# Sums of four pairs of states, new slot counts and a new order in a layer of attention, experts and a state-space mixer on Trainium2

## The chip, the cores and the metric

The kernel runs on one core of one Trainium2 chip. A core has five engines with a queue of instructions each: PE (matrix products, with PEld for the loading of weights beside it), DVE (vector), ACT (scalar), POOL (GpSimd) and SP, which here only issues DMA transfers. 16 DMA engines move data between the chip's main memory (DRAM) and the on-chip memory SBUF; PE writes its results to a second on-chip memory, PSUM. The metric is the time of one execution on the device, in microseconds (us); lower is better.

## The reference

The input x has 16 sequences of 256 tokens of 128 numbers. Four sublayers follow, each added to x:

```python
x = x + attention(layernorm(x), w_in, b_in, w_out, b_out)
x = x + ffn(layernorm(x), gate_w, w1, w2)
x = x + mixer(layernorm(x), W_x, W_dt, b_dt, A_log, D, W_out, b_out)
x = x + ffn(layernorm(x), gate_w, w1, w2)          # the same weights again
```

In `attention` the softmax weights `att[b, l, m, h]` sum to 1 over m, and they are used in `einsum('blmh,blhd->blhd', att, v)`, where nothing else depends on m. So only v, w_out and the biases matter.

`ffn` sends each token to the two best of 8 experts:

```python
top_vals, top_idx = top_k(x @ gate_w, 2)
top_w = softmax(top_vals)
h = relu(einsum('td,edf->etf', x, w1))             # 128 -> 512
expert_out = einsum('etf,efd->etd', h, w2)         # 512 -> 128
final = einsum('etd,te->td', expert_out, combine)  # combine: top_w at the two experts
```

`mixer` is a selective scan with 16 states n per channel d. With delta, B and C made from x by products with W_x and W_dt:

```python
dA_cumsum = exp(sum over later positions of delta * A[d, n])
xs = cumsum(delta * u * B[n] * dA_cumsum) / (dA_cumsum + 1e-12)
y = sum over n of xs * C[n] + u * D
out = y @ W_out + b_out
```

All is in 32-bit floats.

## The kernel before

The 4,096 tokens are cut into eight blocks of 512 (`TB`). A block goes through attention, the gate, its experts, the mixer, a second gate, its experts and the output. For the experts the blocks are put together in sets: in the first layer [0], [1], [2,3], [4,5], [6,7] (`FIRST`), in the second [0,1], [2,3], [4,5], [6], [7] (`SECOND`).

**Routing.** For each set, a buffer `slots` in DRAM has room for `SLOTS` tokens per expert: the first number of a layer's tuple for a set of one block, the second for a set of two. `route` counts each token's place in its expert, and POOL scatters the weighted rows there with indirect transfers (L807). If an expert had more tokens than there is room for, a general version of the whole computation would run after the planned one (`general`, behind a branch at the end). With the reference's inputs the fullest expert has 142 tokens in the single sets of layer 1, 310 in the double ones, 318 in the double sets of layer 2 and 176 in the single ones.

**Experts.** `divided` turns the room into chunks: at most 128 tokens to a chunk, all chunks of one size. 330 tokens are 3 chunks of 110. For each expert of a set, `experts` fetches its tokens from `slots` as a tile `xs` of [chunk, number of chunks, 128] with one transfer from SP's queue. It transposes them on PE to `xsT`, does four products with `w1_s` into the banks `ps_b`, relu on ACT or DVE into `h`, four products with `w2_s` into `ps_y`, transposes back and stores `yr` in the buffer `ys` in DRAM with another transfer from SP's queue. There are four buffers each for `xs` and `yr`. Every row that such a transfer moves is 512 bytes long. So each layer has 40 fetches and 40 stores. When a set's stores have landed, POOL gathers the rows for each token into `yy` (`collect`, L821), and they are added to x.

**Mixer.** One call does a block. For each pair of states, ACT makes `decay` and `th` (two exponentials and tanh for the two states, 512 columns each), PE spreads B and C over the partitions into `ps_B` and `ps_C` from three bf16 pieces, DVE multiplies (`ps_B`), scans (`w`) and multiplies with C and `w` into `th`, which holds two states of 512 columns:

```python
            group.append(th)
            if len(group) > 1:
                product(group[0], group[0], th, ALU.add)
            if len(group) == ADD:
                for k in range(2):
                    matmul(so, wsh_s, group[0][:, k, :], False, n + k == NS - 1)
                group = []
```

With `ADD` = 2, two such tiles are added up on POOL or DVE and then multiplied with W_out (`wsh_s`) into the bank `ps_s`: four groups in a block, 8 products of 512 columns. A product of 32-bit floats shows as two records on PE.

**The order.** Nothing here is issued in the order of the program text. Every operation becomes a job of a `Plan`, with the engines that may do it (`either` offers two for many: POOL or DVE for `product`, ACT or DVE for copies and relu) and an assumed duration from `cost`, `matmul`, `transpose` or `move`. `Plan.forward` plays the jobs through with these durations, picks by a rank for each job, which the packed string `ORDER` holds, and so decides the engine, the buffers and the place of each instruction. What comes out is a fixed sequence for each engine. The engines then follow their sequences, each waiting on semaphores for what it needs. All operations made by these helpers carry L710 in the profile.

Of the kernel before, what the change touches and what calls it, by code (L numbers as in the profile page):

```python
# [40 lines left out]
XN, ROW, XS, XT, H, YT, DEPTH = 4, 3, 4, 3, 4, 3, 3  # L41

ORDER = (
    "c-oy;3zS?{m92a3_kHWtzxw}AcS6!hI-~;z$O;57;6V8Q2_u0S5d^_uSc)<WMU9}iM3yW-9GO9x!6gH;R9KFnMgszpL;?f?f"
    "k*<R^Xq@t@4Y*x(n)u9Rdv$gbywAU_uY5jJ?HGR&pu3!7%XbbZAPKv1@3dL7-PWr9y>~ce89&%(C@K%Jo9!(hVu?i`7ck&TU"
    "=}!eF%Vl)_8eOGlzoV+GCP40*uyj))&`!j{^V`L0}L96gZ<4gs;O)2b>A*3(6>rA1qHftKE)g1PD&+d4C53zj>tYtuRmST4)"
    "&WZ=i;-Wdt8&k}Jkz4frZfW0dx>2F9<qDP7bBq>YMzaZlQu8;l;?+ePSH#x<oKoEc04YdQ9_z#2UcR8YkQZ@_JKUIwrXpCBw"
    "y%n$|z+H*Fet87`^C*_nH1fcC_oYqiEa5-i%s&Llw`v@46X#t7>ItB=v6B`tD>z8D<E*H}0f-#>loAIJY14hsV+|<5QxV>F6"
    ">MACb|KehA*xQaiirRK`r;~{cLjneDt0Nf|kEoo*U@p9_j!i#dWsezvrR+sxshv)zuWsGhFh-7pml~U+|6RMg#e{BnBi1OJ8"
    "{AtKz1A~GTIhQXQRn%ke_1+;3-()<bWZJRR6xkpvtH^UoJyCT1TFBd-vKZw{l=N5^8I7n;k;oMd;@Ct0ds)?$Q&UmPXz}F6#"  # L50
    "dW9?-*SWOvxor10@uUMTT|4)h($^?t#9+p%<8@UwC4u_H&;{uTgXsAMiMbl@4dSA0RXZ4ACKM^vhG!qIZ3nF^_^|>`d-Tn&K"
    "wyzk<LlLQRB1Sh~zY_bopU;AF}%AS(s#+{Wm8iwK;{49U2`nGz1AY|+UEUrmJ%G;LyF9NZ`WH88wyQ>luGWVmKT3OV<!#{EW"
    "z!NIr5>A!W@A}UR$AWI|yFk+BEncN=R!(&QNPwlz&?wY>(L5$Xj@WkfMZ5@g#l8cWfdX#yell3CZhJqETdv4Sl?uKS~-)v})"
    "*4Vd22ckBKk|8VVy=0BLVS=}uE1S@ZYfgCSgm>u8<lgqPqc<;kc?rNJurWMKMhvbR2qEm+|2UcJKs<96Vvpuj0d3D4Ol{~jD"
    "cbd9cbIWM858=Cz7YhCRBII%{;(YO>*0hKYgrutqLc+%P%RBi3%*?jzD0>I3<3Efd@<bwI+I<3KauaD-H2gE37^e)@TEs7Rl"
    "mCTe(M@e{Hq2=o>!CxJnq#en9mpN*lS+&Iw2j!+`ts4{f2PVMHH#yYYq^BZsi=|-|t8(JfC6;{iqKJpA{YQK>8{db}Y7%1%m"
    "$WPD1#pR5Rju3=MF*JyEdPx|=W?&I655)808;G9f7ezWWA3XfwvOg@aHMUvd&5l5TnkS>p^$u;L$4aYP5jbo}#ADG_H0DKuj"
    "u!Z7tjkurLfov96nM^nzTX@8{Q$937vRW0C-5uOb^Oj3%l#B4<#!j~c5E#e_fwC;J+RCpwK|NPft1JPleU~<FVRNIdf6eaz_"
    "Nv0P>Z+A!CEICH}&6*u~1??PyUf7eg8@uY%b;<r%k|>f-k1T$sZg1Me)YxXVdWNeW?%8tuHdp{3#ogBbYA;w0bivzZvubm=S"
    ";u|tWYNdXxF6B#=HHK)3%~O5?RK;+SsOX+qgTI%sagY#bZ33c{lh?fXeo(UeK9XlQ!l>}&R7jB33OpT{afUf*+^D_6L!6*c<"  # L60
    "h7L9m@!!-^s_fy|QfmDvDt?3h}Vp{*$OLDcCS%nsc8svmPfsu)&;TDFcKF;EU}a@<8*34~xXDg|A}%sHpKTeo9dE`>kiXNE!"
    "2}Rao~0CdHr>Vh5vv;!0oyH0!d8k45OvgXmyL7+J<Yl^FG(U|O>XL3Z^p+mWlK0Gj2vl>bFE98-Xh<|d<ttXm_ycw_46$d*="
    "N{H*TW<G$1MvHzy|X*oCAKl|_DUET4E2{EZ~6~SV(+hdkJ2eiw&E}+CZo)u}D7<-j8X)h}#*5`2TRY(d%ak`I(om3YX7XQ;-"
    "82r-(aOFxjFT(DFH3&d<{WUmyg<*(gK;*T8E51PH6`c5O%$++arQY0k=N}_YL3^ZMXC|Hk8Tkp7kug{EMoc)KVA>SNEd*jOR"
    "9YC!pixRCZz|TuC8>TjE2Sd2j>|k}_jex`*77FX%xVN5;iP64HL+aT94Q(>1jRGe9_6W#Uzmtbw}b7x^s&|tS_9HVKCt5A<r"
    ";K3#2~{Q$LJJ~Hs`_xjttq@*ZSwWyjf2SC@AZj@tRoMK)SD!2#kI>vgzGf`??{<_J?ayD>|GN-@g6sACYC`O>cGby6Yag{&{"
    "i}+$XP#SP|(-qF~Kw%fXLgv}ls@Vcf(y{7%z2MX{bU?!9o?c~7re&u%04nm5av&iTz*iXBTg#+qYc$6S5>Z_diGZg@Lf6Z@l"
    ")wW4G;Y_;oS5sUq}{^J@BankP?#tvB!n0-i|(&S41wf@8QeqzI@v|6^xKn>E_@SbQwN(5yWll87$l4ZQ+dV~^R$DnXlPzYRo"
    ")nh#23O4sr7AdIyNKVav-OU8V&iXsz8B^JL-v%twpAwQ=Qp|pL-T}0+fY4v3M`J_Ct2}NOAeM^U#$*H;)v^arT5v56Py~LZy"
    "KtG#Z#A8=wV{w6{Aq2UK4;F$;&&I4XD{lhb2fGEE&R*a#-{EVssn+QktixhOrgXABzgXo6auRe$x$=KXq4BsUH~Xp{8b1kln"  # L70
    "N+6lChLhmik8mt@M}Y;tMZR#K=n$X_u5IpFss8+P{mW+v!LiI0f_TD5d!MEHHWJ{fMhI2>AeM8WT~lFC&MDJMTtfyM<#FVQG"
    "6lvYlzEg5Xy?ijwILJC0%|7jEaAdM4HQ9Ul^>ZtxO2d*7_vQ`_~SaB^+CfzpN?51RLemBMwz*BO@dmSRRDbMiV)Q)90R8v)z"
    "PHZ9pW?~U#))Iqb7HGfO(OYbK0V2jtFoI3HtT9vb*jfliR`xD_|=fpUst#pJqUfuD|?7`1i9dy4PmcQ6C_ua2TI`NL#X@*mg"
    "FRefEuh)`e$Qz<7@yzC)%_k#wz7<VN(?nT?jN!h38#$$@B&A}fNhKD)_V3C>6?W_Km;UG4d2i226s4(^Prc~oj9DzqGETcK8"
    "l1I%Z`po^mmqr`!`l4Z+3U}RBpKnhl}a~$D~2#N!gR!o$meVKHLX;2^h2XY87cFhMkAv)*fxxquK9mk7i_+QICRJ`ksSbxqM"
    "*I8qi^KK9B8|S>`kad*b*wWhc}`O7B-;)d)e~yQKVGI!z@(HG(2T0$>Pb^WShXEOR;`2lv#Y9kQb>_Ogj2i=fq_yU67CeVZr"
    "{@gsGEVbJj_oU$d>DPTCh!;?-g}h~-P|d6M0v5E0K_4$xYQ1gxnot`W$KR~PH@`L`l|7UC;<sTQxWUQ6||poTy22!i!IhKzy"
    "pXQf3l-Gg!A-@Dv~rsY^rO)gVE@UZZmD)VdP0}msHuac5QY{JGYJL#qvpHEjmiedOSa1F&HY|ulVc)O@cHts`I{@eiBjwR(!"
    "_8ix^k!l0(h~&T7vM4e5KVN*DYOK3E+dhbWdb3?O^7)&A1eAW?=7Vz!2K8hi*_g1DL}BPd81oY)3j%rzwa6$#het4-Ihzya7"
    "77H$j6raj9Caxc6jsy)rla2BZ#kLR!ussM?-TivyE_K=-%6eQ%Dy}IKPmF8KGQE(BPY{&sD0aUkypJowK$5&pz3Zxld!;r4b"  # L80
    "i{@8#QJ_IFn*;{VzcdLVpURg@j=$V-dy;p8g9$&<0E*5r}RnW4ssP!0vkwhv!q5M?mqtJQ-&7z$ANdJr>3`CNU5J!(3K065A"
    "i+L-$}&JeEnTAef=kA}-sw&-e>J#HChX&52<yMomPBiDcydpfxkF<esn+mybj<nYg@AEfou;>8oatI$$gl&*zUTVA&_w=>d0"
    ")VuxalN-e>{1?hHd#T<gEY603Sq;ya#Gqh_Mm3NVtcv12paWEAp@N;jl_QKli;?LCjg<s`!{TB$IU6ISyA=LpWVI7x57}ZFu"
    "UyR@ii5A&vj>Y+kR=nMcOp1blceu7K&ZmLJKbnmXE#R8F_*sih9<z#X+;A%6{A{Ez$^$XzqzsgPamGSd;v$zQUxv|TBU}pJO"
    "amc?{~0On8j*%t>`(S5uz_(gF0ig2eO`~@C)l`YfsL7i$mXvUPy{QQMzyN>t{N*$*BV(<B)RH{Zi?qJ-47zZD6A6QTNl6PX5"
    "ISpC}NRp5Pnd{WL_F(JZ&*EA26kJwh%tbQBz`jL{MqK*a1OmW2Y&=;)dCIpY+M<9hn6WW0SGk%=for-_rsND|HXUrYeDY^Wt"
    "uRc9iXm1sqF%8mqwdiz%BgB3yFq0D1xK{)d$SD=|z!!`R#$kn*RmVr&^uNvVT^94rO$#9JszL!=M5ANyV03eex*#vqAJ5%Ny"
    "4jqAju=(&N=4uCL$VU#40LZNbPG?#1NILG;DwkqZqSz2uCi;rN@$1`Lu><|JJbQm8p-oY1<G0KV!2gME%*-8+W+2sVI7iO}V"
    "by#4#`*ZG+D5_>`9E(B_QH4OGPsRbTmB)28Dj{m%J|AhKbS}aVhfpCwQ3T%8MPLEt0_hZ!m=-&iwY`GPJ764^K~`KA)|>;ZT"
    "@}ro$BSFRTs>(OgIUG3@gF-FYys&tR|0K7L5=Q1R;Acpqk2X^1mlt)<4r;#9V#Ar;xBaY8bA8LwH`k|bnD=W9={Cqp~?6mho"  # L90
    "&4_Wy<Nnt3%6`4o`d?Jc7`~W)6IU(A0xWeYE66moHm&C{%Swf1)8>zM4L0V)e(guDC4q`lQj5u0A+aaZ8un3Qd1Ymv1sxdPR"
    "bXpF`2ny4=hvZmZ(jB1TFvQ!y*3d@871G&uZwjyQCLcvtak_0a06QK|H{u2@M=iF$eXLNf~A_>t8mIX5}CBwCXxTAHI}2I<h"
    "`E~}xkx}PS^I0)w{z$;7M(mMgE@bH1*P=z1LhC|cMJ}fL|GOVkadMHZ|Iwe#A`toNgp%6N%#M5OoJ7Xx|oBi^Al<r1{j)cBY"
    "l~?L1sL<2Fxe}N<G+K_!DGWB1<tAJ`9fwY^rJe?ox=L6Hjs_FgT9+F+bp=uascEUaWHugt_1Qsn0t`Y``6H-EgwhO|E(3LFi"
    "Z?4fSLUZ9QdC9!r$s_l{2aE7_!YHqVmIU{%F`z!%!=I%kKZ5%&Cmzc%b~}~q>IM!rb81tqy!K!VUCYqq#7$!!==bhCX=3s;$"
    "%^*;wCa3OO-O9o(ZQ-hqNQio)L;mia^O(WxDCmOmSION~THP!{KuJTjQtx^z2P$M2bgM$Pd4pP-rZqEAXmI7_yZA^bv5zLiv"
    "(<9@0~Uc6m5-C3WfQIGd(iPb1aJH#rlw)TN|RU9cU3796-NOrQ-8{Em$WuY$d&)W2z2U6(ZvewlXCrKM0GRTY^=ugp-!=%Y&"
    "Fsu8My`l0<!hGyKW_?@eYMLo3~SMyobTC68?dK%$h)m{3q^-@n)MyH}zA67bsj(WIKz)be3x{NFe<qcAG^{A`%9Fy8f&&*3R"
# [1408 lines left out]
```

## Time and profile before

| | |
|---|---|
| time, median of 9 runs | 794.86 us |
| lowest and highest | 791.75 and 800.44 us |
| the profiled execution's own time | 793.23 us |
| its span, first to last instruction | 791.5 us |
| mean granted clock of TensorE | 0.885 |

The profile is of one execution. Its page gives the busy time of each engine, the DMA queues (q1 is SP's, q0 that of POOL's indirect transfers), the groups of instructions (line, engine, operation, output<-inputs, shapes, count, busy time in us, mean duration in ns, idle time before them and what ended it) and who waited for whom. A table of stretches gives, for any two moments, the busy time and number of instructions of each engine, the granted clock, the mean busy share of the 16 DMA engines and the GB/s that they moved. A timeline lists the instructions in order of time: start, duration, engine, operation, count.

### The profile page before, as it was taken

The numbers are of one execution on the slowest core, as the hardware profiler recorded it, in microseconds if no ns is written. First come the engines' busy times: TensorE is split into PE (matmuls) and PEld (weight loads), VectorE is DVE, ScalarE is ACT, GpSimd is POOL, SyncE is SP. The second block draws the span as 40 slices with busy tenths as digits, with TensorE's granted clock in tenths as the row PEclk, the third lists the DMA queues.
The fourth block names the chain that finished last, engine by engine and source line by source line (L and its number), as shares of the span: only waits on it lengthen the run. The fifth ranks groups of instructions, "written<-read, shape, count | busy, mean of one in ns | idle before, by whom it ended". The sixth has DMA issues, their size and how long they took to land. (4 is left out here: it accounts for less than half of the span.)

```text
span 791.5 us, 8786 instructions
## 1 busy us (share of the span) xinstructions
PE 647.5 (82%) x2598; PEld 402.3 (51%) x2598; DVE 555.2 (70%) x1038; ACT 487.5 (62%) x996; POOL 414.5 (52%) x490
## 2 busy tenths in 40 slices
...
GB/s 242 330 50 59 76 79 34 61 47 60 77 76 18 9 18 49 109 61 34 27 69 82 46 20 64 21 59 40 35 50 90 123 41 70 65 59 96 43 94 96
DMA packets 76373, 55.05 MB, mean 70 GB/s; under 512 B 8064, under 2 KB 69152, under 8 KB 76320
## 3 DMA queue, kind: packets, MB, share of 16 engines
q1 hardware_dynamic: 66464, 37.35, 16.2%
q0 software_dynamic: 8192, 16.79, 7.2%
...
q14 instruction: 31, 0.25, 0.1%
...
## 5 line engine op out<-in xcount | busy, mean ns | idle before, releaser
L710 PE MATMUL ps_b<-xsT,w_s 128*128 128x330 f32 (+3 forms) x640 | 221.2, 456 | 34.5 <-issue 14.0
L710 PE MATMUL ps_y<-h,w_s 128*128 128x330 f32 (+3 forms) x640 | 218.1, 431 | 7.2 <-ACT yT L710 5.4
L821 POOL DMA_INDIRECT yy<-ys,of x128 | 124.5, 973 | 123.1 <-DMA ys<-yr 59.4
L710 ACT ACTIVATE h<-ps_b 128x384 f32<-128x384 f32 (+2 forms) x234 | 110.1, 476 | 119.3 <-PE ps_b L710 77.3
L807 POOL DMA_INDIRECT slots<-row,to x128 | 126.8, 991 | 100.7 <-issue 23.3
L710 PEld LDWEIGHTS ps_b<-xsT,w_s 128*128 128x128 f32 x640 | 120.0, 205 | 98.8 <-issue 29.4
L710 DVE TENSOR_TENSOR_SCAN w<-decay,ps_B 128x1024 f32<-128x1024 f32 x64 | 145.8, 2278 | 0.2
L710 PEld LDWEIGHTS ps_y<-h,w_s 128*128 128x128 f32 x640 | 112.4, 199 | 49.9 <-issue 13.9
L710 DVE TENSOR_TENSOR ps_B<-du,ps_B 128x1024 f32<-128x1024 f32 x64 | 78.2, 1222 | 44.8 <-PE ps_B L710 34.2
L710 ACT ACTIVATE th<-later,lneps,ha_s 128x512 f32<-128x512 f32 x128 | 100.0, 809 | 2.9 <-DVE th L710 1.9
L710 ACT ACTIVATE decay<-delta,nea 128x510 f32<-128x510 f32 x128 | 86.7, 714 | 4.8 <-DVE w L710 3.8
L710 DVE SCALAR_TENSOR_TENSOR ps_C<-th,ps_C 128x1024 f32<-128x1024 f32 x56 | 68.3, 1220 | 12.8 <-PE ps_C L710 11.7
L710 PE MATMUL ps_s<-th,wsh_s 128*128 128x512 f32 x128 | 69.8, 637 | 4.4 <-POOL th L710 4.3
L710 DVE TENSOR_TENSOR th<-ps_C,w 128x1024 f32<-128x1024 f32 x56 | 67.9, 1213 | 0.2
L710 POOL TENSOR_TENSOR th<-th,th 128x1024 f32<-128x1024 f32 x20 | 47.2, 2358 | 33.8 <-DVE th L710 25.4
L710 PE MATMUL ps_b<-ident,xs 110*128 110x110 f32 (+3 forms) x208 | 40.5, 287 | 21.8 <-issue 11.9
L710 POOL TENSOR_TENSOR rstd<-var,root 128x8 f32<-128x8 f32 (+1 forms) x20 | 28.2, 1413 | 56.7 <-DVE var L710 54.0
L710 PEld LDWEIGHTS <-sel 96*128 96x128 bf16 x256 | 26.3, 104 | 59.6 <-issue 49.6
L710 PE MATMUL ps_b<-ident,yT 128*110 128x128 f32 (+3 forms) x208 | 45.0, 287 | 9.5 <-ACT yT L710 4.1
L710 ACT COPY yr<-ps_b 110x384 f32<-110x384 f32 (+3 forms) x68 | 29.7, 440 | 34.4 <-remote 17.3
L710 PE MATMUL ps_B<-pieces,sel 96*128 96x512 bf16 x128 | 42.5, 405 | 10.1 <-DVE w L710 9.8
L710 PEld LDWEIGHTS ps_b<-ident,xs 110*128 110x128 f32 (+3 forms) x208 | 27.3, 152 | 42.1 <-issue 19.0
...
## 6 DMA issues: line engine op xcount, KB each, us to landing
...
slots<-row,to POOLq DMA_INDIRECT x128
```

Source lines behind the costliest of these rows:

```text
L710: return lambda: f(*[real(x) for x in a], **{n: real(x) for n, x in k.items()})
L807: inst = nc.gpsimd.indirect_dma_start(out=real(out), out_offset=bass.IndirectOffsetOnAxis(ap=real(rows), axis=0), in_=real(in_), in_offset ...
L821: nc.gpsimd.indirect_dma_start(out=real(out), out_offset=None, in_=real(in_), in_offset=bass.IndirectOffsetOnAxis(ap=real(rows), axis=0), ...
```

## The change

It has four parts. `ADD` goes from 2 to 4, so that the tiles of four pairs are added up before the two products with W_out. A branch for `ADD` equal to half the number of states is added. The assumed durations of DVE's short and fast instructions and of PE's short products are changed. `SLOTS` gets new numbers, and `ORDER` new ranks.

```diff
-SLOTS = ((192, 330, 480, 632), (216, 384, 600, 800))
+SLOTS = ((184, 336, 480, 632), (200, 380, 600, 800))
 UNIT = 2
-ADD = 2
+ADD = 4
...
 ORDER = (
...
     def cost(engine, name, views):
         n = max(v.free_size() for v in views)
         if engine == "DVE":
-            t = 0.15 + 0.00208 * n if "scan" in name and n > NE else max(0.2, 0.15 + 0.00104 * n)
-            return t + 0.08 * sum(v.free_size() == 1 for v in views[1:] if n > 1)
+            out, *ins = views
+            ins = [v for v in ins if v.free_size() > 1]
+            fast = name in ("tensor_scalar", "tensor_copy") and not any(
+                v.home.psum or v.dtype != F32 for v in (out, *ins)
+            )
+            t = 0.15 + (0.00208 if "scan" in name and n > NE else 0.00052 if fast else 0.00104) * n
+            return t + 0.07 * sum(v.free_size() == 1 for v in views[1:] if n > 1)
...
     def matmul(out, lhsT, rhs, start=True, stop=True, **order):
         n = rhs.free_size()
-        took = max(0.25 if n <= 16 else 0.42, 0.00178 * n) if rhs.dtype == F32 else max(0.06, 0.00044 * n)
+        took = max(0.23 if n > 16 else 0.2, 0.0017 * n) if rhs.dtype == F32 else max(0.06, 0.00044 * n)
...
             group.append(th)
             if len(group) > 1:
                 product(group[0], group[0], th, ALU.add)
-            if len(group) == ADD:
+            if len(group) == ADD == NS // 2:
+                product(group[0][:, 0, :], group[0][:, 0, :], group[0][:, 1, :], ALU.add)
+                matmul(so, wsh_s, group[0][:, 0, :], False, True)
+            elif len(group) == ADD:
                 for k in range(2):
                     matmul(so, wsh_s, group[0][:, k, :], False, n + k == NS - 1)
                 group = []
```

Through `divided`, the new `SLOTS` give these shapes of the tiles that are fetched and stored, and of the products' columns:

| sets | room before | as chunks | room after | as chunks |
|---|---|---|---|---|
| layer 1, one block (2) | 192 | 96 x 2 | 184 | 92 x 2 |
| layer 1, two blocks (3) | 330 | 110 x 3 | 336 | 112 x 3 |
| layer 2, two blocks (3) | 384 | 128 x 3 | 380, rounded up to 381 | 127 x 3 |
| layer 2, one block (2) | 216 | 108 x 2 | 200 | 100 x 2 |

The sequences that come out differ on every engine. In the sums of `th`, POOL has 32 instead of 20 and DVE 16 instead of 12. The products into `ps_s` from `th` are 32 instead of 64. On SP, the fetches of the second layer's set [2,3] stand behind all eight stores of [0,1] instead of between them.

More of the change, by code (lines that the diff above doesn't have):

```diff
@@ L43 @@
 ORDER = (
[L44 to L98, printed above, removed]
@@ L99 @@
-    "YdmMxAO$n(YeN$ybbOaV6%8^2zS1*j2oGzV{zTp1(Yv#Z&O`qXwp16!"
+    "c-pmBX^>pib?$r4-QL!(x7qg%?K{?r09g`if$Rc|SuC(q?1fd1g9tGO65Eu6j46i%CzcH^Qzq6An_whxAOsU9LWVL(2FoHw2"
+    "pB+v_F21oy8GRnH<G58>CuR!(o-`%@4ma7d(L;h^BpJ1<vo;AIYMt21z{ZIU<<jAd&Y2+h9<^_WlD_fZ%Q`{5RyNCc&_AMe?"
+    "ET&YP?#$d9YgqoV#w2T?uv?0Rh-=T4g~rFfd#}PB9ELdNB4W*kF(e1jcD1a?TNfXSv{BKd1K$XkgBYZwmmsp?}_svJhP59{A"
+    "uTOgf&HLL*laB%d~$VFEcr+RZ|FCT(@wOkgcs2#ySO6nzQS&2tzoWn`Y<igO@C<SkclsH1Zv+7?%IHo#w;jkt)T0nm~RS_)i"
+    "FzYWkO>i`o%NI|ya>P^5CTm^JNq=_~ca^1~B_<)k5D^PKlY;R7w^J`z3pWVOAwqeu;krz&kGY(7^6kU!Mvp{NX!TVO7B`iC3"
@@ new lines @@
+    "=s#CB9Bg_O8X0%}*zT5(+xwxO4LGr6_p`N!8#B<r4kntTu~&wCD`0EnbKZ59?eniD2b)ImO4u5|Ky6Nr)adwPwpXmQoCnU?w"
+    "f1dxK6_=3*Jb^%EA1t4Chv>KqL$y)@+jSM*`<ApWKNP1Ji8Ee8oA^={kujC_$*@rrGh|H<iWRvut4z)(>!C#FvvVX?n=^hA%"
+    ";+DHA0V}KRAfS-wP33xT0rZBSoZZa9-28?SQuA2DuSJi<yWxu!TdHYROTYErGZZwD`LR5!Q0T2{@r03y_OHJS=b}xry8zS6p"
+    "lc;4f?dhyf3HG|3&oTUlIq8$h)qT?f}N&dHyMk=sz5DJX6%hK!3EhS;_N<;9GGik?CWByBp|vaI@n+H|h1maJD~9telvfQ*4"
+    "f5kim@A?en2KLd$+VNd6Kx2~@}(oqX3R)}X)`vy~k(?PJn%hp6+A5I*bNhju<d}7JZkJa=~N5NRl$l`?O-JgyQpUH-puLc_W"
@@ new lines @@
+    "YL84CwzDi5AF5T`+xuEP(7=+Jg!5WX*^QE5=;TsbNEKyd`@G$21S_bmR{$@_0WQ%UwMH9Kqr)|XN7(yjH;4SnEYJMwObS*@K"
+    "FHTt(&Cv+wh4OP<GPl%vvfW{RS2}Q3VCY}H<ScHptQ`BCqW7vOFzs4w?umE+F|a6L*y-$i#@(?sD7(IEZaB#^eflW%B}l<{9"
+    "#8lR}h^?I)A-F*nFMkSiobrrwuLd7Jr~dKK3MIvexD@E-lgLxKZye#%%G0Z48{{f(xSyO8K64&SlKwckZFtt#ny~Nx7aUrH)"
+    "239>4y58g>O!7Dt((SFssD0LtA(88pw!S}u6FSW+mvz$pIA5yph&7KGvyHsx5-jvCE(zrdNCrUJo)5l+Yn4n-Fid@lXblAY6"
+    "YA1?h)s-L$#o6O`cx<cuoU~;B`NQxLj*Att-C?g~gY?$K`5@4qlb%pKMyq9r0dOQCl1PWj4-E9Y&^Wedd6La(%3*K1pE+k>d"
@@ new lines @@
+    "TBMyPXYE<}2X+>`8lB63nUGG>wLf63>}XWB@7ALVVJ3UaUENiC$L5=UbPu}`pHg@G&iOyQW%I-G8|?nBFD6tIpV>_ovqy+;W"
+    "|1knCpq|zy==|g+&5LKN7z?cTW*(k|NVxS;YR#{zSY0$vZpTV!%N|}-W)Cd@=H&w&q5D-$7}H9?wVuq0qA7=M2Dqg@?VliQ("
+    "4xIA2>;M&>L|_SOe_Wvvh3h8GC#7!<pg@HLJ#Yyy-||8dt&YXnVqr^Qfl+BOb300n*nh0;6&|4=zH+hs&M>?sKtx$Lj>e#nB"
+    "<Fe<Nx>DB`($69f82*Dpv$RYf|4Fbz64jYENJguHkzrH7h0D@a0r!R3l73snM+il~JPS_WgK1Q|WC{5!lh_{PgkFa1_P?t(9"
+    "l^nQzD{-I^P^Iqua4cceK()We|^H@kY$TPLJ9pVP@Ynt5HC_<D0c5%YJq5+|v;Y>?M%D_#DLC5yQwL~TS!Dksn7ZMu@VNjuE"
@@ new lines @@
+    "`S0_fPA<D$hl>q1aidw>i}9Z@=+-NLK)hE^HOTm*qFa#FHR00Ot%Ts&Zcf#azd9W{m(Z;F$j|8D<=%{VqdH&QwxH!Aa)J?Rj"
+    "-Bx5^t!c!^KX!rYGBdml6Kn-f>9pW0=*%m!V(QPG12gbT7%$C;#0fcjC-CNt@l6Pd|%glOZ#CqycKQn|E=**GqN+-yMD@ZUa"
+    "UKklB^T<=~hc_r}`6TZEzqFcVivmyQ%(EN)jPPGxfU?1F3qZS>9GHvmVddn1n9&j@?{0|3Q`4DK-oCMBCjNzTFd-Irab%92G"
+    ")f-8k+2{CP^Yf3%Az)zSy+lRv-W%-0tmgcj^=^5ZYA{*ToMA<p_eOWFHc_IDlTb?7H&+s-{LAGc293t^`>&9XiG$vew_w*uS"
+    "PhhD<o*|V=}gw;czuCbigTJ|>&Kr{Q$tylJr*g%X^mF)8!&8b%Sp}P2WEUZ5Ti>d`=8wLWZQd09}+qvJQP!9Y;7Qk3JIOoyY"
@@ new lines @@
+    "(SdqBIMS-~@j$>p>u4^?FIQ;C>d?w<5yXxt3Lf?lW8CCq;_(&8b5@I5<_jVP!R;ZnN={>S6oC}g5ZT~$9BRQ!Hty<syZh)!Y"
+    "(`)%nS0>Kw?TE>JO59!_mJMn`lH^JHH>vAf)eQ{G&R~LfG~^S(!y9>D+v-qBInu=_KPuS!=0aEjLi?TK?mws()QYR0F}2pFC"
+    "@IK(t#tR$Q!v6vttaJaql%m)>n2Mlr)@lg@EWvf}7a#74pOl;)!~R#=dD&QjrWXF0Ocp;GC9Yg%)e+uG}J!@}<wvk#CR`Gm`"
+    "06WhDit0eCH{2fH6p^_f4rOewYY#ndr%+4)h!(=Zw&r86M8g-E=XFX#}HgrXb3A~ATsth*FF+3|6|)AM2TTNq}ZO7(hKJHzY"
+    "PL0-%CZmS>#q@w+?xGi@atI5wGo;Q9bmFRZ<X)viefOYiB8R~^&sdOjI$K7hS<2;#(yFQy+`$}6|z1rjtCFa^Q)$g4dwvKYC"
@@ new lines @@
+    "2?sLphIMmDPi*0?UkHycJbaZKp9Rg^)MwisAex(pagkBB`i(c5Y?X81Ew^3T+X~8FoQSa@JJA&X*3pjlZ)EMfx2r~}vu2;Wc"
+    "lO@(9d$Kn?deB{;v+YZkS)YU>a89Bb<S(ok(T7~OpU)i?PTVQS~w7mYw40cB6q;A+_YIy2ntcAa-LSiY%XVk11wM^1OxpBQC"
+    "b}@P>H6JBfUkgYfI&m`0Lf0IF;@bG8B@iMfbwzA8Bpa^;e(XI`E^0{P1J(eT`T5ylXw&zO8k6@>nokSSmW7bGrsqYKUm5zZs"
+    "*`)SSExxg`ve%PHK(&g$y~nYNU6<u6=9B4-8ZFGtl85-dwB4`smHKPA!9s03h4h;`Dn?IZ?k`8As;)mL#v>}SNVAG2bY0$Zx"
+    "Ceux}>JsQUm1@%kf(}fF&YWaIlqtF*LHA&NYp!tAIN?63$*>b~1s=S+V6Ja-D?d=p6_5quT4N1Fi>E$;c9ldi~yq_}T?iGjL"
@@ new lines @@
+    "JMSNsW<L7z9|h)YQQvU5@RB)XI<URBZIv@kil{wm#R;mEkp{&}f{zjlq#Z%o)y*BCkcd#|4ap?;4uzoz{m9T!;=gUrSrxn-T"
+    "Ycc^+H=Kc8gftU=zN!X-M!dO#s7>x|H#$LNJkKs$QMTUJESlE27{QD`2yLlsZAh1QVPeo{BkIj`oBc|gey}t%$(UuO6z*YlK"
+    "B1mKss>}^>sp%Qbvn^UFJ1zSx1e<9SGDr8P(sMN~()wkl>H4W2|X?Sgu5%K5JWwWS-IXmhVwUEs+L0C_Y2dchSZ`@cw_K;k8"
+    "!Y^0>uYfgtWtrc%Q&C^}cAzBY2scioI};Xctacx6LFHr@HOt%xu8QloVSahn995=CcNQkX&t14ekJhUbq=n^Y*GDfEn9`q36"
+    "gJD{Ay$|L9Mu>6K@1Uo7gE!aRB^Wy7t^wM}R+`dH3+31ZzPt)6t?QU+gJ-$y}yoB_04c#K(Or#UOW!DjQ;DS$+(;5|V48drv"
@@ new lines @@
+    "Z*h`vaX_`20NKL>8MX6v&Y|Y6lLr>|+`&*S03iyRi8`c?EF>AR=rJPtdg)LbVsN02+65B-$i06jO-~fd<HV!eJWoKkHLB6yN"
+    "k*q+Ac62QtZfH7+_Y=={g^H^KNPs(upLFbhc?0QCG5kq`mg!b$PE+%ifL2b$b#Be8*(G_FOO%kN%0gfgo1!FmejXa3UkyD7P"
+    "Jf<6LTDC=`eaQ5_W=yYel`IvVGtBXBn7V8jr{a$>(?NitYb=lEEwzs$t>hKEzxQUriydIUXO2M688E-MEzD$`H&FHR)_Rik-"
+    "KP;U(0-fVfrENWO#^`#b9aE<tcucmYm5Fu)o2fLKFaQrHtyXG>B+&G~Ca$^c1Ag|oO#3(vlf!E_=RjyaMRV3Yec)n>EPo~h~"
+    "A=TZ|yzFrviAS|F2wjgV%WuW3n`9ZM3utz5+(t{W#8wtDATvPKz4SlZ94}v8z`{;AjZPYg%(`VH)aKpx$6a}F<>~enAP8tRv"
```

11 lines of the change are left out of this document (added).

## Prediction

> **What bounds the kernel now.** I read the page first, its busy times and then its DMA lines.
>
> ```profile
> span 791.5 us, 8786 instructions
> PE 647.5 (82%) x2598; PEld 402.3 (51%) x2598; DVE 555.2 (70%) x1038; ACT 487.5 (62%) x996; POOL 414.5 (52%) x490
> ...
> DMA packets 76373, 55.05 MB, mean 70 GB/s; under 512 B 8064, under 2 KB 69152, under 8 KB 76320
> ...
> q1 hardware_dynamic: 66464, 37.35, 16.2%
> q0 software_dynamic: 8192, 16.79, 7.2%
> ```
>
> The span is 791.5 us and the profiled execution took 793.23 us, 1.7 us more; the median of nine runs is 794.86. PE is busiest, and in 400 to 710 us it is busy for 275 of 310 us beside a DVE with 249. The DMA queues look idle: q1, SP's queue, takes 16.2% of 16 engines. That share is a mean over 16 engines, and the change touches how many of them one transfer uses. So I counted q1's packets. Its data are rows of 512 bytes: 47,328 for the fetches and stores of the experts (twice 24 x 384 + 24 x 330 + 16 x 216 + 16 x 192), 9,216 for the blank fills, 4,096 for half of the weights; and 3,072 rows of 2 KB for the other half, xT and the output. Together 63,712. The remaining 2,752 fit one completion packet for each engine that a transfer uses. The 35 transfers with 128 partitions or 3,072 rows use 16 engines, 560 packets, and so do those with 128 and 96 partitions among the experts' (2 x (24 + 16) x 16 = 1,280). This leaves 912 = 48a + 32b for 110 and 108 partitions: a = 11 and b = 12, the largest divisors of 110 and 108 that are at most 16. With 16 engines for all it would have been 3,120. Next, the table of stretches, asked for the middle of single transfers: stores from 110 partitions (first row), 128 (second), 108 (third), and the full queue early in the kernel. The last two columns are the DMA share of 16 engines and GB/s.
>
> ```profile
> 302.95:303.75 0.80, 0.80 (x5) 0.59 (x4) 0.43 (x1) 0.18 (x1) 0.77 (x1) 1.00 0.68 171
> 477.85:478.40 0.55, 0.55 (x2) 0.21 (x2) 0.55 (x2) 0.55 (x2) 0.00 (x0) 1.00 1.02 290
> 740.10:740.70 0.60, 0.60 (x3) 0.58 (x3) 0.00 (x0) 0.27 (x2) 0.00 (x0) 0.50 0.57 155
> 20.00:36.00 16.00, 7.96 (x35) 6.26 (x34) 11.24 (x73) 3.71 (x12) 5.74 (x5) 0.50 1.10 334
> ```
>
> The share is 0.68, which is 11 of 16, where 110 partitions move, and full with 128. 108 stays under its 12 of 16. A transfer is cut into equal shares of its partitions, so an engine count has to divide them. One engine moves 290 / 16 = 18.1 GB/s.
>
> **The change: the transfers.** The new slots give 92, 112, 100 and 127 partitions (184/2, 336/3, 200/2, 380/3 rounded up). Divisors up to 16: 92 has 4, 112 has 16, 100 has 10, and 127, a prime, has 1. So the 24 fetches and 24 stores of the second layer's three double sets, 381 x 512 = 195,072 bytes each, go from 16 engines to one. At 18.1 GB/s that is 10.8 us for each, where before it was 0.7. Bounds: 334 GB/s at a share of 1.10 is 19.0 GB/s for one engine, so 10.3 us; 171 GB/s at 0.68 is 15.7, so 12.4 us. I take 10.8, from the store of nearly the same size. All 48: 518 us (494 to 595).
>
> The Trainium skill, "DMA: Bandwidth & Descriptors", section "Why a DMA increments its semaphore by 16 and not by 1", states the same divisor rule, names 127 partitions as a case with one engine, and adds that on the hardware queues it is always the lowest-numbered ones; no row here shows which engine is taken. [...]
>
> When they run, the SP timeline shows (start, length from first to last, operation, count):
>
> ```profile
> 400.81 2.61 SPq L710 DMA_DIRECT2D xs<-slots  x4
> ...
> 512.93 5.57 SPq L710 DMA_DIRECT2D xs<-slots  x5
> ...
> 610.00 2.56 SPq L710 DMA_DIRECT2D xs<-slots  x4
> ...
> 713.04 0.57 SPq L710 DMA_DIRECT2D ys<-yr  x1
> ```
>
> The sets [0,1], [2,3] and [4,5] start at 401, 513 and 610, and the last store of [4,5] is issued at 713. So 518 us of transfers stand where there are 312 us. One queue, q1, carries all of them, and I assume that its shares are dealt from the same first engine each time: then the 48 run one after the other and set the pace.
>
> The sum goes stage by stage. In the new order PE meets the first of these experts after 64 of the 128 ps_B products instead of 70. Two ps_B cost DVE 1.22 + 2.28 + 1.22 + 1.21 = 5.9 us, so the first fetch moves from 401 to about 384. Then 518. On the same engine also run the indirect transfers: q0 takes 7.2% of 16 x 791.5 us for 256 issues, 0.22 us per issue and engine; some 130 issues lie in this stretch, 29 us. Another 30 or so transfers of other sets at 0.5 us give 15. The last store has landed at 384 + 518 + 44 = 946. What covers what: a set's 8 fetches (86 us) delay its experts, and its stores (86 us) run beside the mixers of later blocks. PE and DVE, with 275 and 249 us of work in that stretch, are no longer last, so what they do is hidden in the 518. SP's queue is passed in order, so the stores of layer 1's set [6,7], issued between the first fetches, wait behind them, and POOL, which gathers them, waits with all that is queued on it: the sums of states, rstd and the next gathers.
>
> ```profile
> POOL yy L821 <- DMA ys<-yr: 59.4, 5, 20.3
> ```
>
> This wait grows by some 60 us at one place, beside the transfers and not on top of them. From the last store's issue to the end it was 791.5 - 713.0 = 78 us; some of the single set [6]'s experts can go while PE waits, about 15 us, and [7]'s fetches queue behind the last store, 8 us: 71. Hence 946 + 71 - 11 (landing instead of issue) = 1006 of span, 1008 of time. I say 1010 because idle gaps of the engine between sets can only add.
>
> **The other transfers.** First layer, single sets: 16 to 4 engines, 46 packets on an engine instead of 12; at 512 B / 18.1 GB/s = 28.3 ns this is 0.96 us for each of 32, on the path at a set's first fetch and last store, 4 places: +4 (0 to 31). Double sets, 11 to 16: 30 to 21 packets, -0.25 us, hidden by four buffers: 0 to -1.5. 12 to 10 engines with 200 rows: 18 to 20 packets, nothing.
>
> **The change: the sums.** Each mixer has two groups of four pairs instead of four of two; the new branch for a group of eight is not entered, since ADD is 4 and NS // 2 is 8.
>
> ```profile
> L710 PE MATMUL ps_s<-th,wsh_s 128*128 128x512 f32 x128 | 69.8, 637 | 4.4 <-POOL th L710 4.3
> L710 POOL TENSOR_TENSOR th<-th,th 128x1024 f32<-128x1024 f32 x20 | 47.2, 2358 | 33.8 <-DVE th L710 25.4
> ```
>
> Half of these 128 records go: -34.9 us of PE. Sums rise from 32 to 48; by the order of instructions 12 more go to POOL (12 x 2.36 = 28.3) and 4 to DVE (4 x 1.22 = 4.9). Eleven other additions and products of 512 columns move from POOL (-14.3 at 1.3) to DVE (+7.5 at 0.68). So POOL and DVE get about +13 each. In the chain of waits PE's ps_s has 2.6% of the span, 20.6 us, of which half would go: -10. DVE runs at 36 to 38 of 40 us in the stretches from 280 to 440, so its 13 can come back in full: -10 to +13, I take -5. PE columns: 16 fewer in 256 records and 8 fewer in 256, at 0.8 ns a column (498 ns at 384, 349 at 192 for ps_y) -4.9 us, against +1.8 for 336 and -0.9 for 381: -4 of PE, -2 on the path. The new ranks change which work meets which, and no row prices this: PE is idle for 144 of 791.5 us, and I allow a tenth of that, 14 us, either way. Of all this only what lies before 384 us counts in the forecast, since the transfers cover the rest: half of -5, and +4 for 92 partitions, nothing in sum.
>
> **Rivals.** First, each transfer uses one engine, but a different one each time. Then they overlap, and only their latency is longer by 10 us: at the first fetch and the last store of three sets, 6 x 10 = 60, less 8 for the sums: about 845. For it: no row names an engine; against it: one queue, one sequence. Second, on the other side: 127 partitions are cut some other way into enough shares (over the three rows of each partition: 3 engines, 3.6 us each, 48 x 3.6 = 173 us in 312) and hidden; then the sums' -5, the columns' -2 and +4 for 92 partitions leave 793 - 3 = 790, and with the ranks 776 to 804. It decides from about 5.6 us per transfer down, where 48 and the 44 us of others fit into the 312 us. Against it: 110 partitions by 3 rows got 11 engines, although their 330 rows would divide by 15. Third, the transfers are hidden and the sums don't bring what they are meant to, because DVE's +13 comes back in full where its stretches are full already: 793 + 13 - 2 + 4 = 808.
>
> **Numbers.** Same engine each time: 0.85, centre 1010; its own range goes from 494 us with 25 beside it (384 + 494 + 25 + 71 - 11 = 963) to 595 with 20 us of gaps (384 + 595 + 44 + 71 - 12 + 20 = 1102). Another engine each time: 0.08, 820 to 870. Hidden: 0.06, of which faster than now 0.04 and within 0.5% (about what a measurement of this kernel can tell from no change) 0.02. Hidden with DVE as the bound: 0.01. Slower is 0.85 + 0.08 + 0.01 = 0.94. The range leaves out all but the first case (0.15) and a little at its upper end; its lower end is drawn out to 930 for the case that some transfers still pass each other.
>
> **What would show it.** q1's packets: 63,088 of data plus 560 + 2 x (24 x 1 + 24 x 16 + 16 x 10 + 16 x 4) = 1,824 completions, 64,912; with 16 engines for all it would be 66,208. Long stretches after 385 us with a DMA share near 1/16 and some 18 GB/s; PE waiting for xs<-slots, POOL's wait for ys<-yr several times 59 us. ps_s records 64. I am wrong if q1 counts more than 65,000 packets, or if the share in these stretches is well above 0.1 and the time below 900.

## The result, and the profile after

The changed kernel takes 1022.86 us (median of 10 runs, 1020.67 to 1025.39), the kernel before 794.84 us (31 runs): the ratio is 1.288, with a 95% interval of 1.284 to 1.291. The forecast was 1010 (930 to 1100). The profiled execution took 1022.93 us, with a span of 1021.2 us.

The page first: the busy times, SP's queue, and the chain that ended last, by engine.

```profile
span 1021.2 us, 8695 instructions
...
PE 666.1 (65%) x2534; PEld 414.4 (41%) x2534; DVE 567.2 (56%) x1060; ACT 489.4 (48%) x989; POOL 429.5 (42%) x499
...
q1 hardware_dynamic: 64912, 37.03, 12.5%
...
PE 39%; DMA 27%; DVE 9%; ACT 8%; issue 8%; POOL 5%; another core or an unknown queue 2%; SPq 1%; ACTq 0%; POOLq 0%; DVEq 0%
```

No engine is much busier than before in microseconds, yet the span is 230 us longer, and DMA has 27% of the chain, 276 us, where before it had 1%. Queue q1 looks idler than before, 12.5% against 16.2%: the mean over 16 engines hides that one of them does the work. What gives it away is q1's count of packets, 64,912: it is the count with one completion for each of the 48 transfers of 127 partitions. With 16 for each of these it would be 720 more, 65,632.

The list of waits (total, times, longest, in us), and three groups of instructions (busy, mean ns of one, idle time before them and what ended it):

```profile
PE ps_b L710 <- DMA xs<-slots: 134.6, 17, 28.4
...
POOL yy L826 <- DMA ys<-yr: 104.3, 5, 49.7
```

```profile
L710 POOL TENSOR_TENSOR th<-th,th 128x1024 f32<-128x1024 f32 x32 | 75.3, 2354 | 167.1 <-DVE th L710 109.0
L710 PE MATMUL ps_b<-ident,xs 112*128 112x112 f32 (+3 forms) x208 | 46.1, 314 | 146.4 <-DMA xs<-slots 134.6
...
L710 PE MATMUL ps_s<-th,wsh_s 128*128 128x512 f32 x64 | 42.0, 758 | 18.5 <-POOL th L710 18.5
```

PE now waits 135 us for rows of the experts; the list of before has no such line. The products by W_out are halved to 64 records as announced, and POOL has 12 more sums; both are beside the point here.

SP's timeline (start, length from first to last, operation, count), from the first fetch of layer 2's double sets to their last store:

```profile
410.24 28.25 SPq L710 DMA_DIRECT2D xs<-slots  x4
...
480.31 128.86 SPq L710 DMA_DIRECT2D ys<-yr  x9
616.69 72.69 SPq L710 DMA_DIRECT2D xs<-slots  x8
689.78 48.09 SPq L710 DMA_DIRECT2D ys<-yr  x5
737.99 38.03 SPq L710 DMA_DIRECT2D xs<-slots  x4
...
786.02 8.90 SPq L710 DMA_DIRECT2D out_T<-xnT  x1
...
934.39 1.57 SPq L710 DMA_DIRECT2D ys<-yr  x2
```

Before, four such issues took 2.6 us together. Now SP is held while what it handed over earlier drains: the four fetches from 737.99 on are issued without a pause between them, and 38.03 us is 9.5 us each. (A row's length also holds SP's own pauses: of the 48.09 us of five stores it is idle for 15.) The sets start at 410, 617 and 738 instead of 401, 513 and 610, and the last store of 381 rows is issued at 935. Two stretches inside (PE, PEld, DVE, ACT, POOL busy, clock, DMA share, GB/s):

```profile
560.00:600.00 40.00, 25.08 (x60) 8.83 (x59) 35.57 (x61) 22.51 (x39) 22.59 (x24) 0.66 0.07 21
...
800.00:840.00 40.00, 18.26 (x56) 10.15 (x54) 7.41 (x10) 8.54 (x17) 2.34 (x3) 0.70 0.08 22
```

At 800 to 840 us every engine is half idle or worse, and the DMA engines move 22 GB/s: a share of 0.08, little more than 1/16.

### The profile page after: what moved, and what is told of

Same layout as the page of the kernel before. It is cut to its first block, busy times and chain, and to the rows that moved or that the text cites. A ratio compares the mean times of both kernels' runs of the same rounds, so it can differ in the third digit from the quotient of the medians.

```text
span 1021.2 us, 8695 instructions
## 1 busy us (share of the span) xinstructions
PE 666.1 (65%) x2534; PEld 414.4 (41%) x2534; DVE 567.2 (56%) x1060; ACT 489.4 (48%) x989; POOL 429.5 (42%) x499
## 3 DMA queue, kind: packets, MB, share of 16 engines
q1 hardware_dynamic: 64912, 37.03, 12.5%
## 4 chain that ended last, share of the span: by engine, by line
PE 39%; DMA 27%; DVE 9%; ACT 8%; issue 8%; POOL 5%; another core or an unknown queue 2%; SPq 1%; ACTq 0%; POOLq 0%; DVEq 0%
PE ps_b L710 23%; DMA xs<-slots 20%; PE ps_y L710 12%; DMA ys<-yr 5%; DVE w L710 2%; PE ps_s L710 2%; ACT decay L710 2%; PE ps_B L710 2%; POOL slots L812 1%; DMA yy<-ys,of 1%; ACT th L710 1%; SPq L710 1%; PE ps_C L710 1%; POOL yy L826 1%
## 5 line engine op out<-in xcount | busy, mean ns | idle before, releaser
L710 PE MATMUL ps_b<-xsT,w_s 128*128 128x336 f32 (+3 forms) x640 | 225.5, 467 | 36.4 <-issue 13.9
L710 PE MATMUL ps_y<-h,w_s 128*128 128x336 f32 (+3 forms) x640 | 230.4, 454 | 4.5 <-issue 3.0
L710 ACT ACTIVATE h<-ps_b 128x336 f32<-128x336 f32 (+3 forms) x239 | 112.2, 473 | 140.0 <-PE ps_b L710 109.0
L710 PEld LDWEIGHTS ps_y<-h,w_s 128*128 128x128 f32 x640 | 119.9, 212 | 69.7 <-issue 42.0
L710 POOL TENSOR_TENSOR th<-th,th 128x1024 f32<-128x1024 f32 x32 | 75.3, 2354 | 167.1 <-DVE th L710 109.0
L710 PE MATMUL ps_b<-ident,xs 112*128 112x112 f32 (+3 forms) x208 | 46.1, 314 | 146.4 <-DMA xs<-slots 134.6
L710 PEld LDWEIGHTS ps_b<-ident,xs 112*128 112x128 f32 (+3 forms) x208 | 29.8, 166 | 171.7 <-issue 146.0
L710 ACT COPY xsT<-ps_b 128x336 f32<-128x336 f32 (+3 forms) x66 | 26.7, 409 | 151.2 <-PE ps_b L710 118.5
L710 PE MATMUL ps_C<-pieces,sel 96*128 96x512 bf16 x128 | 47.0, 443 | 20.6 <-DVE th L710 20.4
L710 PE MATMUL ps_s<-th,wsh_s 128*128 128x512 f32 x64 | 42.0, 758 | 18.5 <-POOL th L710 18.5
```

What stands on the lines that cost most here:

```text
L710: return lambda: f(*[real(x) for x in a], **{n: real(x) for n, x in k.items()})
```

## The experiments

They ran in three sets, each with its own runs of the kernel before, which took 726, 798 and 724 us there; so only ratios to before within a set are compared, and expectations given in microseconds of the first measurement are read as ratios to 795.

| Kernel | Ratio to before | 95% interval | Before in its set |
|---|---|---|---|
| after, with 384 for 380 | 1.025 | 1.022 to 1.028 | 726 |
| before, with 380 for 384 | 1.310 | 1.304 to 1.315 | 726 |
| after, each transfer of 127 partitions cut in 112 + 15 | 1.028 | 1.023 to 1.034 | 726 |
| after, with 366 (122 partitions) for 380 | 1.094 | 1.087 to 1.100 | 726 |
| after, unchanged | 1.278 | 1.272 to 1.285 | 798 |
| before, unchanged | 0.998 | 0.993 to 1.004 | 798 |
| after, with all slots of before (sums, costs, ranks) | 1.017 | 1.012 to 1.022 | 798 |
| before, with 184, 336 and 200 (384 kept) | 1.015 | 1.011 to 1.020 | 798 |
| before, with the sums of four alone | 1.037 | 1.032 to 1.042 | 724 |
| after's costs and ranks alone | 1.031 | 1.026 to 1.037 | 724 |
| before, with 336 alone | 1.011 | 1.006 to 1.015 | 724 |
| before, with 160, 336 and 192, 336 | 0.999 | 0.996 to 1.002 | 724 |

### Is it the 127 partitions?

Two kernels are complements: the change without its 380, and its 380 without the change.

```diff
-SLOTS = ((184, 336, 480, 632), (200, 380, 600, 800))
+SLOTS = ((184, 336, 480, 632), (200, 384, 600, 800))
```

> The changed kernel with 384 slots instead of 380 in the second layer's double sets (chunks of 128 x 3), all else as changed. Theory (127 partitions put each of 48 transfers on one DMA engine, and that engine sets the pace): 16 engines again, so the 228 us go and what is left is the net of the sums, the other slots and the ranks: 776 to 804 us, q1 with 64912 + 24 x 2 x 15 completion packets + 2 x 24 x 3 rows = 65776 packets. Rival 1 (the new ranks or the longer sums on POOL cost the time): stays near 1020. Rival 2 (381 is an odd number of columns, and products, copies or relu on it are slow): also about 790, so this run doesn't part it from the theory.

It takes 743.69 us (742.32 to 746.0) beside 725.65 of before: 1.025. Nearly all of the loss is gone, and so is PE's wait:

```profile
PE ps_b L710 <- DMA xs<-slots: 1.8, 3, 1.0
```

But the remainder is slower than before, not 3 us faster as my terms for the other parts had it; 1.025 is above the 0.976 to 1.011 expected here.

```diff
-SLOTS = ((192, 330, 480, 632), (216, 384, 600, 800))
+SLOTS = ((192, 330, 480, 632), (216, 380, 600, 800))
```

> The kernel before with 380 slots instead of 384 in the second layer's double sets, all else as before (ADD = 2, old ranks, old other slots). Theory: the first fetch comes at 401 us, then 48 transfers of 9.6 us (the spacing of the fetches in the changed kernel's timeline) = 461, with 50 us of gaps and others, and 80 to the end: 980 to 1030 us. Rival 1 (ranks or sums): stays near 795.

It takes 950.36 us beside the same 725.65: 1.310. In microseconds this is below what was expected, as before itself is faster in this set; as a ratio it is at the upper end of the theory's 1.23 to 1.30, and slightly over. Its waits have the changed kernel's form:

```profile
POOL yy L821 <- DMA ys<-yr: 166.0, 5, 87.5
PE ps_b L710 <- DMA xs<-slots: 157.3, 14, 38.9
```

So one digit in the slots, which takes work away (three rows in 384), costs 31% by itself.

### Is it the odd width, or the number of engines?

Theory: the count of engines is the largest divisor of the partitions up to 16. Rival: something else about 381 rows or 127 columns. The first kernel keeps all that is odd, and only cuts each transfer at partition 112:

```diff
+        if cut == 127:
+
+            def emit():
+                for p in (slice(0, 112), slice(112, 127)):
+                    e.dma_start(out=real(out[p]), in_=real(in_[p]))
```

> The changed kernel, in which each fetch and each store of a tile with 127 partitions is issued as two transfers, of partitions 0 to 111 and 112 to 126 (divisors 16 and 15). Everything that computes keeps its 381 columns. Theory: no transfer is on one engine any more; the time is that of the run with 384 slots, plus up to 10 us for 48 more issues of 0.6 us on SP: 780 to 815. Rival 2 (odd width): stays above 950.

It takes 744.05 us, a ratio of 1.028, the same as with 384 within the intervals (and, as that one, a little above its range, 0.981 to 1.025). q1 counts 66,352 packets: 31 completions for each of the 48 where the changed kernel has one. The products with 381 columns and the buffers of 127 partitions are still there; they cost nothing that these runs can show. SP's timeline, where the eight fetches of the second set are now sixteen:

```profile
524.44 26.55 SPq L807 DMA_DIRECT2D xs<-slots  x16
```

Sixteen issues take 26.55 us, SP's pauses included, and none is longer than 0.9 us; the changed kernel's eight took 72.69 without a pause.

The other kernel changes the count of engines by one:

```diff
-SLOTS = ((184, 336, 480, 632), (200, 380, 600, 800))
+SLOTS = ((184, 336, 480, 632), (200, 366, 600, 800))
```

> The changed kernel with 366 slots in the second layer's double sets: chunks of 122 x 3, and 122 has 2 as its largest divisor up to 16. Theory, with the same engines each time: 183 rows on an engine, 183 x 25 ns = 4.6 us per transfer, 48 x 4.6 = 220 us where there were 312: no longer the pace of the whole, but each set's fetches and stores in a burst still wait: 800 to 850. If every us of transfer time counted in full it would be 48 x (9.6 - 4.6) = 240 less than the changed kernel only down to the floor near 785. Rival 3 (one or two engines, but different ones each time): transfers overlap, 785 to 800.

It takes 797.42 us, 1.094: between one engine (1.310 in before) and sixteen (1.025). It is above the theory's range too, 1.006 to 1.069 as a ratio, but 0.025 stands with sixteen engines as well, which the theory didn't count; it is far above the 1.006 at most of rival 3. The page's line for q1, and SP's timeline:

```profile
q1 hardware_dynamic: 64240, 36.66, 15.9%
```

```profile
535.33 35.04 SPq L710 DMA_DIRECT2D xs<-slots  x8
```

The count is that of two engines: 64,912, less 48 x 15 rows, plus 48 completions, is 64,240. Eight fetches take 35.04 us, half of 72.69.

### The repeat, and the other parts

The kernels of before and after, unchanged, in the second set:

> The kernel before, unchanged, for a trace on the chip on which the experiments run: there its median was 725.65 us beside the first four of them, where the first profile's execution took 793.23. Every theory expects 724 to 730 us; the trace is to show where the 68 us between the two executions of one program lie. If they are spread over stalls of PE, idle time of PE falls from 144 to about 80 us and the durations of single instructions stay.

> The changed kernel, unchanged, on the chip of the experiments. Theory (48 transfers of 9.6 us in a row set the pace from the first fetch on): the stretch of transfers, about 525 us, does not shrink with the rest; what lies before and after it does, by about 10%: (1023 - 525) x 0.91 + 525 = 978. If all shrinks alike: 0.913 x 1022.86 = 934. Between them: 930 to 980.

Before took 794.90 us here and not 724 to 730, so where the 68 us lie could not be seen, and whether the changed kernel shrinks to 930 to 980 us beside a before of 726 stays untested. 1.278 repeats the result, a little below its 1.288.

Then the rest of the change. First all of it but the slots:

```diff
-SLOTS = ((184, 336, 480, 632), (200, 380, 600, 800))
+SLOTS = ((192, 330, 480, 632), (216, 384, 600, 800))
```

> The changed kernel with all slots as before (192, 330, 216, 384): only the sums of four pairs, the assumed durations and the ranks are changed. With 384 slots and the other three changed, the ratio to the kernel before was 1.025. Theory: the sums and ranks cost this and the three other slot counts nothing on balance (+4 for 92 partitions on 4 engines, -2 for the columns): 738 to 744 where the kernel before takes 726. Rival 4 (92 partitions on 4 engines cost it, up to 31 us): 720 to 730.

812.14 us, 1.017, in the theory's range (1.017 to 1.025). And three of the slots in the kernel before:

```diff
-SLOTS = ((192, 330, 480, 632), (216, 384, 600, 800))
+SLOTS = ((184, 336, 480, 632), (200, 384, 600, 800))
```

> The kernel before with three of the four new slot counts (184, 336 and 200; 384 kept): 92 partitions with 4 engines, 112 with 16, 100 with 10. Theory: +4 (0 to 31) for 92, 0 to -1.5 for 112, -2 for the columns: 725 to 731 where the kernel before takes 726. Rival 4: 740 and more.

808.50 us, 1.015: between the theory's 1.007 at most and rival 4's 1.019 at least. Is this the transfers of 92 partitions, on 4 engines instead of 16? The trace says no: with them the kernel is 3 us ahead of before at 140 us, where the single sets of layer 1 are done. It falls behind in steps later, by 5 us at 280 to 330, 5 at 365, 4 at 390 to 412 and 4 at 715 to 723 us, where blocks of two and the last blocks are under way.

Next, sums and ranks apart. The first is before with ADD = 4; the second is after with ADD = 2 and the slots of before. The ranks were carried over job by job.

```diff
-ADD = 2
+ADD = 4
```

> The kernel before with one part of the change: sums of four pairs instead of two (ADD = 4). Slots, costs and the ranks stay those of before; a sum that is new takes the rank of the product ahead of it. Ratios are to the kernel before among the same runs; the prediction's term for this part was -5 us (-10 to +13), that is 0.994 (0.987 to 1.016). Theory 'sums' (in the run that had sums, costs and ranks together, 1.017, a sum of four holds one of the four th buffers longer, the waits of PE's ps_B for w rose from 10 to 21 us and POOL's own for th from 31 to 57): the loss is here, 1.010 to 1.020, with the same two waits high. Theory 'ranks' (the loss is in the new costs and ranks): 0.990 to 1.005 here, and the loss in the next run. Theory 'no owner' (each new order shifts the time by its own amount, within the 14 us = 1.8% that the prediction allowed): anything from 0.982 to 1.018, and the two runs need not multiply to 1.017.

753.32 us, 1.037: above the range of every theory.

> The complement: the changed kernel's costs and ranks with the sums of two pairs (ADD = 2) and all slots of before; the products that are left out give their ranks to none, and the two products by W_out that come back take the rank of the sum ahead of them. Theory 'sums': 0.995 to 1.005, with the wait of ps_B for w near before's 10 us. Theory 'ranks': 1.012 to 1.022. Theory 'no owner': 0.982 to 1.018; together with the run before its product differs from 1.017 by over 0.010.

748.55 us, 1.031: also too high, even for the theory that puts the whole loss here. The third theory alone allowed for what follows from the two: if each part had a price of its own, both would give 1.037 x 1.031 = 1.069, where both together gave 1.017 (and 1.025 with three slots besides, in the set whose before is nearest to this one, 726). So the sums and the ranks have no separate prices: either is worse without the other. The two waits that the first theory named don't tell them apart: POOL's for th is 50.2 us with the sums alone and 49.3 with the ranks alone, PE's of ps_B for w 15.7 and 16.0 (with 336 alone, below: 25.5 and 14.0). In the first of the two the new sums have ranks that I chose; how much of 1.037 is due to that choice is open.

Where each loses can be seen in stretches of 40 and 20 us (columns as above). The kernel with 336 alone, which keeps before's order nearly unchanged, is the yardstick; then the sums alone; then the ranks alone.

```profile
260.00:300.00 40.00, 33.07 (x112) 18.10 (x111) 35.56 (x42) 31.64 (x60) 28.98 (x33) 0.83 0.19 52
300.00:340.00 40.00, 33.71 (x129) 20.77 (x130) 35.17 (x44) 25.54 (x56) 24.96 (x22) 0.87 0.24 66
...
460.00:480.00 20.00, 16.05 (x58) 7.94 (x58) 20.00 (x20) 15.98 (x33) 17.13 (x24) 1.00 0.20 62
...
500.00:520.00 20.00, 16.22 (x53) 7.45 (x52) 18.91 (x33) 19.09 (x33) 9.06 (x6) 1.00 0.14 40
```

```profile
260.00:300.00 40.00, 23.10 (x82) 12.51 (x81) 37.90 (x38) 32.51 (x57) 29.43 (x30) 0.82 0.17 47
300.00:340.00 40.00, 29.11 (x111) 17.68 (x111) 39.21 (x46) 21.89 (x47) 27.58 (x27) 0.84 0.22 66
```

```profile
460.00:480.00 20.00, 11.97 (x36) 5.20 (x35) 17.56 (x16) 14.78 (x33) 4.70 (x2) 0.66 0.00 0
...
500.00:520.00 20.00, 8.24 (x28) 3.22 (x28) 19.14 (x33) 18.23 (x28) 10.38 (x12) 0.67 0.25 73
```

With the sums alone DVE is at 37.90 and 39.21 of 40 us in 260 to 340, and PE, which feeds on it there, does 52 us of work instead of 67. With the new ranks PE has no experts left in 460 to 480 (no byte moves: share 0.00) and works 12 of 20 us, then 8 of 20. These ranks start the first double set of layer 2 early and the second late: their first fetches stand at 366.1 and 506.5, 140 us apart, against 381.4 and 493.7, 112 us, in the yardstick. SP's rows, of the ranks alone and then of the yardstick:

```profile
366.13 2.62 SPq L708 DMA_DIRECT2D xs<-slots  x4
...
506.50 2.56 SPq L708 DMA_DIRECT2D xs<-slots  x4
```

```profile
381.43 2.61 SPq L710 DMA_DIRECT2D xs<-slots  x4
...
493.68 2.61 SPq L710 DMA_DIRECT2D xs<-slots  x4
```

At the end of the gap only mixers remain, and DVE is the busiest engine there (17.56 and 19.14 of 20 us). The changed kernel with 384 has the same gap, 369.0 to 519.7.

The yardstick itself, and the last candidate:

```diff
-SLOTS = ((192, 330, 480, 632), (216, 384, 600, 800))
+SLOTS = ((192, 336, 480, 632), (216, 384, 600, 800))
```

> The kernel before with 336 slots instead of 330 for two blocks of layer 1, and nothing else: 16 engines for 112 partitions instead of 11 for 110. Before with 184, 336 and 200 had given 1.015. By the prediction's terms: columns +1.8 us of PE, half on the path, transfers 0 to -1.5: 1.000 (0.998 to 1.002) if only work and transfers count. Theory 'order' (6 columns change what the scheduler believes of each product, and the order written out shifts; in the trace with 184, 336 and 200 the loss came in steps from 280 us on, where blocks of two are under way): anything from 0.985 to 1.020, with the start times of the states' scans differing from before's in steps and not in proportion to the products. If it gives 1.010 to 1.020, the 1.015 is this edit's; if 0.995 to 1.005, it is that of 184 or 200.

733.68 us, 1.011: the "order" theory's range holds it. Most of the 1.015 of the three slots may be this edit's, which gives the transfers of layer 1 more engines; but the two were in different sets, and the intervals (1.006 to 1.015, 1.011 to 1.020) leave a part for 184 and 200. What in the order makes the 1.1% isn't settled.

```diff
-SLOTS = ((192, 330, 480, 632), (216, 384, 600, 800))
+SLOTS = ((160, 336, 480, 632), (192, 336, 600, 800))
```

> The kernel before with slots that divide into 16 equal shares everywhere: 160 and 336 for layer 1, 192 and 336 for layer 2 (80, 112, 96 and 112 partitions); sums, costs and ranks of before. Theory 'engines and columns': 16 engines for each transfer (330 had 11, 216 had 12), and fewer columns: 0.8 ns x (256 x 32 + 256 x 24 + 384 x 48) less 1.8 = some -24 us of PE, half of it on the path, -12: ratio 0.985 (0.970 to 0.995). q1's packets fall to 2 x (24 x 336 + 24 x 336 + 16 x 192 + 16 x 160) = 43,520 of data for the experts instead of 47,328. Theory 'order' (any other slots shift the order by up to 14 us, and the order of before was searched for its own slots): 0.985 + 0 to 0.018 and more, 0.985 to 1.015.

724.70 us, 0.999 (0.996 to 1.002): above the range of 'engines and columns', inside that of 'order'. Against the kernel with 336 alone, from which it differs in the other three slots, PE's busy time is 610.1 us instead of 629.6 and the time 9.0 us less, so about half of the saved columns come back, as that theory's terms had it. Against before, which has no trace in this set, nothing measurable is left: the gain and the 1.1% of the 336 cancel. No version that was run beats the kernel before.

## Why the prediction was right, and where its sum was off

**One engine for 127 partitions: right.** q1 counts 64,912 packets, to the packet what was worked out, the DMA share in the late stretches is 0.07 to 0.08, and within one set 380 alone takes before to 1.310 while the change with 384 stands at 1.025. The split, which keeps the tiles of 127, and the step with two engines (1.094) show that it is the count of engines and not the prime width. The Trainium skill, "DMA: Bandwidth & Descriptors", section "Why a DMA increments its semaphore by 16 and not by 1", states this divisor rule; the runs with 127, 122 and 128 partitions agree with it.

**The same engine each time, so that the 48 run one after the other: right.** The first rival, with another engine each time, would have let them overlap. In the trace, queued fetches of 381 rows land 9.9 us apart and stores 9.0. A store of layer 1 from 112 partitions, issued at 438.5 us among the first fetches, shows that it is one fixed engine: 15 of its 16 completions come at 450.0 to 450.4, the last at 452.3, just behind the landing of the fetch ahead of it, 451.8. The other engines were free. And the time is not the 845 us of that rival.

**The sum: 1006 of span, measured 1021.2.** Five terms were off, and they cancel to 15 us:

- The first fetch was put at 384 us and came at 410: +26. PE met the first of these experts after 64 ps_B products, as foreseen, where it was 70 before. But the fetch itself stood behind 62 instead of 66: that is four products, 12 us, and not six, 18 us. The rest is that I priced sums, ranks and 92 partitions at "nothing in sum" up to there. The 32nd of DVE's scans over states began at 418.4 us, before at 394.0. With all slots of before (in the 798 us set, where before has it at 398.0) the scan is at 417.9 and the fetch at 409.7, so this delay is that of sums, assumed durations and ranks, not of the slots.
- A transfer took 9.4 us on average, not 10.8. That is 24 to 26 ns for each of its 381 rows of 512 bytes; I had taken 28.3 from the GB/s of a store that lasted 0.55 us in all, start and end included. 47 x 9.4 = 442 where I had 518 - 11 = 507: -65. The lower of my bounds, 10.3, was too high as well.
- q1 moved nothing for 12.3 us at 493 and for 39.2 us at 571, 52 together. I had written that gaps can only add, and allowed 4: they are named in the prediction but not in its sum.
- The rest between first fetch and last store, 525 - 442 - 52 = 31 us, is put down to other transfers and the indirect ones, 44 foreseen: -13.
- From the last store's issue to the end it took 86 us, not 71: +15. These are the 78 us of before and the 8 us of [7]'s queued fetches: [7]'s first fetch is issued 3.4 us after that store (938.7) instead of 3.5 us ahead of it (709.5), and from there it is 82 us to the end in both. The 15 us that I took off, because some of [6]'s experts could go while PE waits, did not come.

Thus the forecast of the last store's issue, 935 us, was hit by luck: two errors of 26 and 52 us stand against two of 65 and 13. The range was right for its terms; the centre owes its closeness to chance.

**POOL's wait: the mechanism right, the size not.** It was to grow by 60 us at one place, and a total of several times 59 us was given as a sign, which did not come. The longest grew from 20.3 to 49.7 us and the total by 45.

**The other transfers: no loss seen.** 92 partitions on 4 engines were given +4 (0 to 31); in before with the new slots the trace is even 3 us ahead where the single sets of layer 1 are done. No run has 92 alone.

**Sums, columns and ranks: wrong in sign.** The sum of these was -3 us, with 14 either way for the ranks; without 127 partitions it is +2.5%. The failed step is that they were added as separate terms: -10 for PE's ps_s, -2 for columns, an allowance for the order. The third rival had named one mechanism, DVE full where its stretches are full already, and the sums alone show such stretches (39.21 of 40 us). The other was not foreseen: which set's experts meet which mixers; the second set's first fetch comes 13 us later. How much of each ratio these two make up was not measured. An allowance of a tenth of PE's idle time was too small for either alone, 1.037 and 1.031. In the change as it is, by the sum above, all of this is hidden behind the one engine, but for the 26 us ahead of the first fetch.
